# Filler work between lattice stretches regrouped, the gate convolution in four rounds, and one-column products spread over the array

## The chip, the cores and the metric

The kernel runs on one core of a Trainium2 chip. The metric is the device time of one execution in microseconds (us), as a median over runs. A core has a matrix engine (TensorE, PE in the profile; its weight loads are PEld), VectorE (DVE), ScalarE (ACT), GpSimd (POOL) and SyncE (SP), which here only issues DMAs. Each engine takes its instructions in the order of its own program, and they meet through semaphores.

## The reference

An image batch x of 32 x 8 x 256 x 256 goes through two layers, each added to its input.

```python
drive = x                        # layer 0 on group-normalised x
grid = drive
for _ in range(15):              # a coupled map lattice
    mapped = 3.9 * grid * (1.0 - grid)
    local = conv3x3(mapped, K_local, groups=8)
    physics = 0.7 * mapped + 0.3 * local
    grid = 0.85 * physics + 0.15 * drive
cml = clip(grid, 0.0001, 0.9999)
h = relu(conv3x3(x, Wp, bp))     # 8 -> 128 channels
nca = sigmoid(conv1x1(h, Wu, bu))
gin = concat([x, cml, nca])      # 24 channels
g = sigmoid(conv1x1(relu(conv3x3(gin, Wg1, bg1)), Wg2, bg2))
return g * cml + (1 - g) * nca
```

Layer 1 quantises its normalised input to whole numbers within 127, with one scale for the whole batch, and convolves it 3x3.

## The kernel before

Phase one does layer 0. Images go in eight groups of four. The lattice of a group is the main thread: for each of the 8 channels, two tiles (s = 0, 1; two images each) take 15 steps. One step of one tile is a **stretch** of TensorE work (`half`, lines 480 to 528), 240 in a group, 1920 in all. A stretch makes four blocks of float32 products, each on 64 x 64 tiles of the array: a diagonal product (low rows to low columns, high to high) and an off-diagonal one, into four blocks of two PSUM units. They go in four parts, in the order of line 501, off-diagonal of one block and diagonal of another in each, and after the first three parts `mark` (line 271) runs a product of one column. VectorE adds the drive (`gt`, line 510) and makes the next map (line 520). Two formats alternate (`m_a`, `m_b`). From `m_a` to `m_b` GpSimd clears edges (line 525); from `m_b` to `m_a` the rows at tile edges are exchanged by two DMAs on SP (`exchange`, lines 469 to 475), which the next stretch of the same tile waits for. A tile's next stretch comes two stretches later.

PE's order is written out by hand. The lattice yields after each stretch, and `together` (line 845) runs other generators in the gap until their yields, scaled by total weights, have caught up with the lattice's. These fillers are:

- `nca` (line 576): for each of 8 strips of an image, eight `hidden` pairs, each twelve products of `im` with `wp_hi` and `wp_lo` into `ph`, one unit of PSUM, and a relu on ScalarE to `h`. A `drain` (line 598) is four float32 products of `h` into `acc`. Per i there are two pairs, each with its own yield, and the drain of the i before. The four loads of the next strip (`rows`, line 561) are issued after the first pair of a strip.
- `gate` (line 705) of the group before: in each of 8 strips, `opened` (four products with `gw2`, then a sigmoid) for the strip before, then the 3x3 convolution of `gin` (x and cml rows, 96 partitions) and `gnc` (nca rows, 48 partitions): five column parts for each, four 32-column products a part, 40 in all (lines 760 to 768). `inputs` (line 656) loads the next strip with three DMAs. The mix, statistics and stores that belong to a strip are `chores`, of which `together` takes one per stretch.
- `prep` (normalising the next group), with products of one column (lines 323 and 356).

`both` (line 861) merges fillers by the same kind of weights; T_NCA, T_GATE, T_PREP and T_LATTICE (line 893) are the sums of the yields.

PSUM has three units of two banks in rotation: a stretch takes two, a pair or a gate strip one; `acc` and `mark` have one bank each. SP's queue holds, in program order, exchanges, up to four background loads or stores of the lattice after each stretch, and what the fillers issue.

Phase two does layer 1 from the stored result. When the lattice of the last group is over, the gate of its four images runs by itself first.

Of the kernel before, what the change touches and what calls it, by code (L numbers as in the profile page):

```python
# [40 lines left out]
P = 128  # L41
# [68 lines left out]
def kernel(  # L110
# [6 lines left out]
    wp: bass.AP,  # L117
    wu: bass.AP,
    wg1: bass.AP,
    wg2: bass.AP,  # L120
    w1: bass.AP,
    bp: bass.AP,
# [20 lines left out]
    grp = cp.tile([P, 4], F32, name="grp")  # L143
    mean_x = cp.tile([P, B, 4], F32, name="mean_x")
    rstd_x = cp.tile([P, B, 4], F32, name="rstd_x")
    gw = cp.tile([96, 2, 3, 32], F32, name="gw")
    gw2 = cp.tile([P, P], F32, name="gw2")
    qw = cp.tile([P, 3, P], BF16, name="qw")
    wp_hi = cp.tile([P, 3, HID], F32R, name="wp_hi")
# [16 lines left out]
    with tc.tile_pool(name="prep", bufs=1) as pp, tc.tile_pool(name="prep2", bufs=2) as pp2:  # L166
        kt = pp.tile([P, K_COLS], F32, name="kt")
        nc.sync.dma_start(kt, konst)
        nc.sync.dma_start(lw, kloc)
        kc = pp.tile([P, 3, P], F32, name="kc")  # L170
        nc.sync.dma_start(kc, kcen)
        nc.sync.dma_start(gw, wg1)
        g2 = pp.tile([P, C], F32, name="g2")
        nc.sync.dma_start(g2, wg2)
        wl = pp.tile([P, 72], F32, name="wl")
        nc.sync.dma_start(wl, w1)
        wp32 = pp.tile([P, 3, HID], F32, name="wp32")
        nc.sync.dma_start(wp32, wp)
        V.tensor_copy(wp_hi, wp32)
        V.tensor_tensor(wp_lo, wp32, wp_hi.bitcast(F32), ALU.subtract)  # L180
        G.memset(wu_z, 0.0)
        nc.sync.dma_start(wu_z[:, 24:32], wu)
        nc.sync.dma_start(bp_sb, bp)
        nc.sync.dma_start(bv, bvec)

        G.memset(zt, 0.0)
        borders = []
        for t, at, n, w, rows in (  # L190
            *((t, 0, 2 * C, W, ((0, 1), (257, 1))) for t in xp_s),
            *((t, j * PART, C, W, ((0, 1), (257, 1))) for t in gs_s for j in range(3)),
            *((t, 0, C, W, ((0, 1), (257, 5), (262, 5), (267, 1))) for t in y_s),
        ):
            k = 64
            for row, m in rows:
                borders.append(
                    (
                        dram_ap(t, at + row * n * w, [[w, m * n], [k, w // k], [1, k]]),
                        zt[: m * n, :k].unsqueeze(1).to_broadcast([m * n, w // k, k]),  # L200
                    )
                )
        for _ in range(2 * NBUF):
            nc.scalar.dma_start(*borders.pop(0))

        V.tensor_copy(masks, kt[:, K_MASK : K_MASK + 2])
        V.tensor_copy(junk, kt[:, K_JUNK : K_JUNK + 2])
        V.tensor_copy(grp, kt[:, K_GRP : K_GRP + 4])
        V.tensor_copy(sel, kt[:, K_SEL : K_SEL + P])
        G.memset(avg, 1.0 / P)  # L210
        G.memset(mhalf, -0.5)

        lin = -R_CML * (1.0 - BETA)
        V.tensor_scalar(kc, kc, lin * (1.0 - EPS_CML), None, ALU.mult)
        for c in range(C):
            V.scalar_tensor_tensor(lw[:, c], lw[:, c], lin * EPS_CML, kc, ALU.mult, ALU.add)

        def blocks(dst, src, off):  # L220

            for dy in range(3):
                t = kt[:, K_M + dy * P : K_M + (dy + 1) * P].rearrange("p (r o) -> p r o", o=C)
                w = src[:, off(dy) : off(dy) + C].unsqueeze(1).to_broadcast([P, 16, C])
                if dy == 0:
                    V.tensor_tensor(dst.rearrange("p (r o) -> p r o", o=C), t, w, ALU.mult)
                else:
                    tmp = pp2.tile([P, P], F32, name="tmp", tag="tmp")
                    V.tensor_tensor(tmp.rearrange("p (r o) -> p r o", o=C), t, w, ALU.mult)
                    V.tensor_tensor(dst, dst, tmp, ALU.add)  # L230

        V.tensor_tensor(
            gw2.rearrange("p (r o) -> p r o", o=C),
            kt[:, K_M + P : K_M + 2 * P].rearrange("p (r o) -> p r o", o=C),
            g2.unsqueeze(1).to_broadcast([P, 16, C]),
            ALU.mult,
        )


        wmax = pp.tile([P, 1], F32, name="wmax")  # L240
        V.tensor_reduce(wmax, wl, AX.X, ALU.max, apply_absolute_value=True)
        wall = pp.tile([P, 1], F32, name="wall")
        G.partition_all_reduce(wall, wmax, P, bass.bass_isa.ReduceOp.max)
        V.reciprocal(sw, wall)
        V.tensor_scalar(sw, sw, MAX_Q, None, ALU.mult)
        V.tensor_scalar(wl, wl, sw, None, ALU.mult)
        V.tensor_scalar(wl, wl, ROUND, ROUND, ALU.add, ALU.subtract)
        V.tensor_scalar(wl, wl, MAX_Q, -MAX_Q, ALU.min, ALU.max)
        for dx in range(3):
            t32 = pp2.tile([P, P], F32, name="t32", tag="t32")  # L250
            blocks(t32, wl, lambda dy: (dy * 3 + dx) * C)
            V.tensor_copy(qw[:, dx, :], t32)


    with ExitStack() as one:
# [12 lines left out]
        def unit():  # L268
            return ps_u.tile([P, 2, 512], F32, name="pt", tag="pt")

        def mark():

            one_ = ps_m.tile([P, 1], F32, name="mark", tag="mark")
            T.matmul(one_[HIGH], qw[HIGH, 0, HIGH], qw[HIGH, 0, 0:1], start=True, stop=True)  # L274

        fixed = lambda shape, name, dt=F32: np_.tile(shape, dt, name=name)
        hi, lo = fixed([P, 2, 2, W], "hi", F32R), fixed([P, 2, 2, W], "lo", F32R)
# [1 line left out]
        for t in ims:  # L279
            for w in (0, PW - 1):  # L280
                G.memset(t[:, :, :, w].bitcast(F32), 0.0)
        TU = 2 * NT
        m_a = [fixed([P, TU, NJ + 2], f"m_a{i}") for i in range(2)]
        m_b = [fixed([P, TU, NJ + 1], f"m_b{i}") for i in range(2)]
# [107 lines left out]
        def lattice(g):  # L392
# [87 lines left out]
            def half(c, step, s, d, m_a, m_b):  # L480
# [17 lines left out]
                    for src, dst, w, rhs in parts:  # L498
                        T.matmul(pt[dst], lw[src, c, w, dst], rhs[src], start=first, stop=not first)  # L499

                for o, dg, first in ((1, 0, True), (3, 2, True), (0, 1, False), (2, 3, False)):
                    blocks(o, False, first)
                    blocks(dg, True, first)
                    if (o, dg) != (2, 3):
                        mark()

                gts = []
                for pt, (ts, w) in zip(two, HALVES):
# [27 lines left out]
            for c in range(C):  # L536
                u = g * C + c
                for step in range(STEPS):
# [5 lines left out]
                    for s in range(2):  # L544
# [5 lines left out]
                            if u + 1 in units:  # L550
                                begin(units[u + 1], s)
                        background(4)
                        yield 2.05

            stored[g] = issued[0] + len(later)
            if g == NG - 1:
# [19 lines left out]
        def nca(b):  # L576
# [16 lines left out]
                S.activation(h.rearrange("p i c -> p (i c)"), ph.rearrange("p i c -> p (i c)"), AF.Relu, bias=bp_sb)  # L593
                return h[:, 0, :], h[:, 1, :]

            pend = done = None

            def drain():
                acc, t, i, hs = pend
                for g in range(4):  # L600
                    T.matmul(  # L601
                        acc[32 * g : 32 * g + 32], wu_z[:, 24 - 8 * i : 56 - 8 * i], hs[4 * g + i],
# [19 lines left out]
            for t in range(NT8):  # L622
                im = ahead
                acc = ps_a.tile([P, 512], F32, name="acc", tag="acc")
                for i in range(4):
                    hs = {}
                    for n in (i, i + 4):
                        hs[n], hs[n + 8] = hidden([im[64 * q : 64 * q + 48, :, n, :] for q in range(2)])
                        if n == 0:
                            if t < NT8 - 1:  # L630
                                ahead = rows(b, t + 1)
                            elif all((b + 1, g) in ready for g in range(4)):
                                loaded[b + 1] = rows(b + 1, 0)
                        yield 1.4
                    if i == 2 and done:
                        nc.sync.dma_start(*done)
                        done = None
                    if pend:
                        done = drain() or done
                    pend = (acc, t, i, hs)  # L640
                    yield 0.9
            done = drain()
            yield 0.9
            nc.sync.dma_start(*done)

        def scales(b):
# [9 lines left out]
        def inputs(b, t):  # L656

            src = gs_s[b % NBUF]
            gin = gip.tile([96, 8, W], F32, name="gin", tag="gin")
            gnc = gip.tile([48, 8, W], F32, name="gnc", tag="gnc")  # L660
            for j, to in enumerate((gin[:48], gin[48:], gnc)):
                nc.sync.dma_start(
                    to, dram_ap(src, j * PART + 32 * t * C * W, [[W, 48], [4 * C * W, 8], [1, W]])
                )
            return gin, gnc

        def blend(b, t):

# [36 lines left out]
        def gate(b):  # L705
# [38 lines left out]
            for t in range(NT8 + 1):  # L744
# [5 lines left out]
                    now["gt"] = opened(two[:, 1, :], last["r1"])  # L750
                    now["was"] = last
                if t < NT8:
                    (gin, gnc), mix = ahead
                    if t < NT8 - 1:
                        now["ahead"] = [inputs(b, t + 1)]
                    elif (b + 1) % GB:
                        staged[b + 1] = [inputs(b + 1, 0)]
                    pa = two[:, 0, :]
                    three = pa.rearrange("p (k w) -> p k w", w=W)
                    for j, src in enumerate((gin, gnc)):  # L760
                        rows_ = src.shape[0]
                        for n, (dx, to, of) in enumerate(PARTS):
                            for i in range(4):
                                T.matmul(  # L764
                                    three[32 * i : 32 * i + 32, :, to],
                                    gw[:rows_, j, dx, :], src[:, i::4, of],
                                    start=(j == 0 and n == 0), stop=(j == 1 and n == len(PARTS) - 1),
                                )
                    r1 = wk.tile([P, 512], F32, name="r1", tag="r1", bufs=1)
                    S.activation(r1, pa, AF.Relu, bias=bv[:, 0:1])  # L770
                    now["r1"], now["t"], now["mix"] = r1, t, mix
# [28 lines left out]
                if sums:  # L800
                    chores.append(sums.pop(0))
                last = now
                yield 2.3 if t < NT8 else 0.9
                while t < NT8 - 1 and len(now.get("ahead", ())) < 2 and chores:
                    chores.pop(0)()
                ahead = now.get("ahead")
# [81 lines left out]
        def after(g, gen):  # L888
# [1 line left out]
            while issued[0] < stored[g]:  # L890
                yield 4.0
            yield from gen
        T_NCA, T_GATE, T_PREP, T_LATTICE = 473.6, 77.2, 4.8, 8 * 30 * 2.05
        for _ in prep(0, ((0,),)):
            pass
        for g in range(NG):
# [181 lines left out]
```

## Time and profile before

| | us |
|---|---|
| median of 3 runs | 12336.9 (12310.65 to 12346.97) |
| the profiled execution | 12344.86 |
| its span, first to last instruction | 12343.1 |
| lattice group 0 (64 to 1533) | 1469 |
| lattice group 2 (2948 to 4371) | 1423 |
| lattice group 7 (10051 to 11379) | 1328 |
| gate after the lattice (11379 to 11769) | 390 |
| phase two (11798 to 12343) | 545 |

Busy time of an engine is the union of its instructions' records. A matmul's end is modelled, so a start is the safer mark. "a <- b: us, times, longest" in a list of waits says how long a sat idle and what ended it. In the timeline each row is a merged run of instructions: start, length, engine, line, operation, tiles, shape and count; a float32 product stands as two records. 64*64 64x320 is 64 rows by 64 columns of weights and 320 moving columns. The costliest groups of matmuls, busy us and mean ns of one:

```profile
L593 ACT ACTIVATE h<-pt,bp_sb 128x1024 f32<-128x1024 f32 x2048 | 2274.2, 1112 | 5042.4 <-PE pt L585 5032.7
L499 PE MATMUL pt<-m_a,lw 64*64 64x325 f32 (+1 forms) x30720 | 2404.9, 432 | 405.2 <-DMA m_a<-m_a 358.0
L585 PE MATMUL pt<-im,wp_hi 48*128 48x512 f32 x12288 | 2627.7, 424 | 144.7 <-ACT h L593 105.2
...
L601 PE MATMUL acc<-h,wu_z 128*32 128x512 f32 x8192 | 1107.0, 611 | 0.0
L764 PE MATMUL pt<-gin,gw 96*32 96x384 f32 (+2 forms) x10240 | 775.6, 452 | 197.2 <-ACT gate L716 181.2
L274 PE MATMUL mark<-qw 64*64 64x1 bf16 x5760 | 946.4, 164 | 0.0
L764 PE MATMUL pt<-gnc,gw 48*32 48x384 f32 (+2 forms) x10240 | 735.3, 430 | 0.0
```

### The profile page before, as it was taken

Reading aid. Unit: us, or ns where it says so; the run is one execution under the profiler, and the core shown is the slowest. Engines: PE = TensorE matmul, PEld = TensorE weight load, DVE = VectorE, ACT = ScalarE, POOL = GpSimd, SP = SyncE. Lnnn points to the kernel's source line nnn. Section 1 sums busy time; section 2 is a strip of 40 time slices with the busy share of each in tenths; the row PEclk is TensorE's granted clock in tenths of the full one; section 3 lists DMA queues with packets and bytes.
Section 4 is the critical chain, followed back from the end, with each engine's and each line's share of the span. In section 5 each row is a group of like instructions: output and inputs, shape, how many; then the busy total and the mean of one; then the engine's idle time right before and its main releaser. Section 6 shows DMA issues by size and latency. Waiting matters only on the chain. (4 is left out here: it accounts for less than half of the span.)

```text
span 12343.1 us, 289997 instructions
## 1 busy us (share of the span) xinstructions
PE 11018.7 (89%) x124192; PEld 6195.1 (50%) x124192; DVE 7823.5 (63%) x11376; ACT 3787.1 (31%) x4034; POOL 1577.6 (13%) x2242
## 2 busy tenths in 40 slices
PE   4888899999999999999999999999999999999854
PEld 2554555555555555555555555555555555555222
DVE  4555666666666666666666666666666666665377
ACT  2222233332333333333333333333333333332133
POOL 1000011111111111111111111111111111111300
PEclk7999999999999999999999999999999999999676
DMA  6545567766777667676776667677667666665988
GB/s 169 98 96 100 102 136 144 144 137 139 142 145 147 137 135 147 144 144 130 147 147 139 133 140 148 135 144 148 134 142 149 137 132 126 125 121 115 201 246 257
DMA packets 2473159, 1759.74 MB, mean 143 GB/s; under 512 B 1021280, under 2 KB 2442944, under 8 KB 2471744
## 3 DMA queue, kind: packets, MB, share of 16 engines
q1 hardware_dynamic: 2380096, 1651.64, 65.1%
q10 hardware_dynamic: 91776, 89.53, 2.3%
q8 instruction: 979, 16.04, 0.6%
q14 instruction: 308, 2.52, 0.1%
HBM read 1130.62 MB, written 473.89 MB: 130 GB/s over the span
## 5 line engine op out<-in xcount | busy, mean ns | idle before, releaser
L593 ACT ACTIVATE h<-pt,bp_sb 128x1024 f32<-128x1024 f32 x2048 | 2274.2, 1112 | 5042.4 <-PE pt L585 5032.7
L499 PE MATMUL pt<-m_a,lw 64*64 64x325 f32 (+1 forms) x30720 | 2404.9, 432 | 405.2 <-DMA m_a<-m_a 358.0
L585 PE MATMUL pt<-im,wp_hi 48*128 48x512 f32 x12288 | 2627.7, 424 | 144.7 <-ACT h L593 105.2
L510 DVE SCALAR_TENSOR_TENSOR gt<-pt,d_b 128x650 f32<-128x650 f32 (+1 forms) x1920 | 1463.6, 763 | 1987.5 <-PE mark L274 1350.7
L510 DVE SCALAR_TENSOR_TENSOR gt<-pt,d_a 128x640 f32<-128x640 f32 (+1 forms) x1920 | 1446.9, 754 | 1608.5 <-PE mark L274 1137.5
L585 PE MATMUL pt<-im,wp_lo 48*128 48x512 f32 x12288 | 2437.3, 393 | 0.0
L499 PE MATMUL pt<-m_b,lw 64*64 64x320 f32 (+1 forms) x30720 | 2305.8, 417 | 111.8 <-DVE gt L510 79.6
L499 PEld LDWEIGHTS pt<-m_a,lw 64*64 64x64 f32 x30720 | 1459.6, 137 | 1193.0 <-issue 511.4
L499 PEld LDWEIGHTS pt<-m_b,lw 64*64 64x64 f32 x30720 | 1380.3, 133 | 903.0 <-issue 451.6
L585 PEld LDWEIGHTS pt<-im,wp_hi 48*128 48x128 f32 x12288 | 1160.8, 185 | 1250.9 <-issue 730.9
L520 DVE SCALAR_TENSOR_TENSOR m_a<-gt 128x640 f32<-128x640 f32 (+1 forms) x1792 | 1429.2, 798 | 58.6
L520 DVE SCALAR_TENSOR_TENSOR m_b<-gt 128x650 f32<-128x650 f32 (+1 forms) x1792 | 1384.3, 774 | 100.6 <-DVE gt L510 1.8
L525 POOL TENSOR_TENSOR m_b<-m_b,junk 128x36 f32<-128x36 f32 x896 | 243.5, 272 | 8070.3 <-DVE m_b L520 5355.6
L585 PEld LDWEIGHTS pt<-im,wp_lo 48*128 48x128 f32 x12288 | 1166.4, 186 | 201.1
L601 PE MATMUL acc<-h,wu_z 128*32 128x512 f32 x8192 | 1107.0, 611 | 0.0
L764 PE MATMUL pt<-gin,gw 96*32 96x384 f32 (+2 forms) x10240 | 775.6, 452 | 197.2 <-ACT gate L716 181.2
L274 PE MATMUL mark<-qw 64*64 64x1 bf16 x5760 | 946.4, 164 | 0.0
L764 PE MATMUL pt<-gnc,gw 48*32 48x384 f32 (+2 forms) x10240 | 735.3, 430 | 0.0
L764 PEld LDWEIGHTS pt<-gin,gw 96*32 96x32 f32 x10240 | 313.3, 115 | 823.7 <-issue 422.0
L687 POOL TENSOR_TENSOR d<-mix 128x256 f32<-128x256 f32 x512 | 554.2, 1099 | 1254.1 <-DVE gate L722 866.6
L274 PEld LDWEIGHTS <-qw 64*64 64x64 bf16 x5760 | 631.5, 110 | 137.0 <-issue 0.6
L764 PEld LDWEIGHTS pt<-gnc,gw 48*32 48x32 f32 x10240 | 295.0, 109 | 423.0 <-issue 416.3
(110 smaller groups left out, 5940.8 us busy)
## 6 DMA issues: line engine op xcount, KB each, us to landing
im<-xp_s SPq DMA_DIRECT2D x1024, 384.0 KB
gin<-gs_s SPq DMA_DIRECT2D x512, 384.0 KB
mix<-gs_s SPq DMA_DIRECT2D x512, 384.0 KB
gnc<-gs_s SPq DMA_DIRECT2D x256, 384.0 KB
d_a<-gs_s SPq DMA_DIRECT2D x2048, 36.0 KB
yb<-y_s ACTq DMA_DIRECT2D x28, 2432.0 KB
xr<-in_x_dram SPq DMA_DIRECT2D x128, 512.0 KB
xp_s<-hi SPq DMA_DIRECT2D x256, 256.0 KB
```

The costliest lines, as they stand in the source:

```text
L274: T.matmul(one_[HIGH], qw[HIGH, 0, HIGH], qw[HIGH, 0, 0:1], start=True, stop=True)
L499: T.matmul(pt[dst], lw[src, c, w, dst], rhs[src], start=first, stop=not first)
L510: V.scalar_tensor_tensor(gt.rearrange("p (u c) -> p u c", u=2), pt[:, :, : w * n], FLOOR, d[:, ts, :].rearrange("p (u t) j -> p u (t j)", ...
L520: V.scalar_tensor_tensor(to, gt, 1.0, gt, ALU.subtract, ALU.mult)
L525: G.tensor_tensor(edge, edge, junk.unsqueeze(1).to_broadcast([P, TU, 2]), ALU.mult)
L585: T.matmul(ph[:, i, :].rearrange("p (h w) -> p h w", w=W), w[64 * i : 64 * i + 48, dx, :], rhs[:, :, dx : dx + W], start=(dx == 0 and w is ...
L593: S.activation(h.rearrange("p i c -> p (i c)"), ph.rearrange("p i c -> p (i c)"), AF.Relu, bias=bp_sb)
L601: T.matmul(acc[32 * g : 32 * g + 32], wu_z[:, 24 - 8 * i : 56 - 8 * i], hs[4 * g + i], start=(i == 0), stop=(i == 3),)
L687: G.tensor_tensor(d[:, cols], mix[:, 1, k], mix[:, 2, k], ALU.subtract)
L764: T.matmul(three[32 * i : 32 * i + 32, :, to], gw[:rows_, j, dx, :], src[:, i::4, of], start=(j == 0 and n == 0), stop=(j == 1 and n == le ...
```

## The change

Four edits go together.

1. Marks: the three one-column products of a stretch run on three tiles of the array, in place of one.
2. `nca`: both pairs of an i are one piece with one yield, and the drains of two i are one piece after every second i. The next strip's loads follow the second pair.
3. Gate: all 128 partitions of `gin` are filled (48 rows of x, 48 of cml, the first 32 of nca). The last 16 nca rows go to `gl`, loaded five times over with the shift in columns already made, so that 48 partitions hold the three shifts and one product replaces five parts: 24 products for 40. `inputs` issues eight DMAs for three.
4. The weights of the yields are changed: 2.4 for a stretch, 2.9 for two pairs, 1.9 for two drains, 4.5 for a gate strip, and the totals with them.

```diff
-        def mark():
+        MARKS = ((HIGH, HIGH), (LOW, LOW), (LOW, HIGH))
+        def mark(n):
+            src, dst = MARKS[n]
             one_ = ps_m.tile([P, 1], F32, name="mark", tag="mark")
-            T.matmul(one_[HIGH], qw[HIGH, 0, HIGH], qw[HIGH, 0, 0:1], start=True, stop=True)
+            T.matmul(one_[dst], qw[src, 0, dst], qw[src, 0, 0:1], start=True, stop=True)
...
+        gls = [fixed([48, 8, W], f"gl{i}") for i in range(2)]
+        for t in gls:
+            for w in (0, W - 1):
+                G.memset(t[:, :, w], 0.0)
...
-                for o, dg, first in ((1, 0, True), (3, 2, True), (0, 1, False), (2, 3, False)):
+                for n_, (o, dg, first) in enumerate(((1, 0, True), (3, 2, True), (0, 1, False), (2, 3, False))):
                     blocks(o, False, first)
                     blocks(dg, True, first)
-                    if (o, dg) != (2, 3):
-                        mark()
+                    if n_ < len(MARKS):
+                        mark(n_)
...
-                        yield 2.05
+                        yield 2.4
...
                     for n in (i, i + 4):
                         hs[n], hs[n + 8] = hidden([im[64 * q : 64 * q + 48, :, n, :] for q in range(2)])
-                        if n == 0:
-                            if t < NT8 - 1:
-                                ahead = rows(b, t + 1)
-                            elif all((b + 1, g) in ready for g in range(4)):
-                                loaded[b + 1] = rows(b + 1, 0)
-                        yield 1.4
-                    if i == 2 and done:
-                        nc.sync.dma_start(*done)
-                        done = None
-                    if pend:
-                        done = drain() or done
-                    pend = (acc, t, i, hs)
-                    yield 0.9
-            done = drain()
-            yield 0.9
+                    pend.append((acc, t, i, hs))
+                    if i == 0:
+                        if t < NT8 - 1:
+                            ahead = rows(b, t + 1)
+                        elif all((b + 1, g) in ready for g in range(4)):
+                            loaded[b + 1] = rows(b + 1, 0)
+                    yield 2.9
+                    if i % 2:
+                        if done:
+                            nc.sync.dma_start(*done)
+                            done = None
+                        while pend:
+                            done = drain(*pend.pop(0))
+                        yield 1.9
...
-            gin = gip.tile([96, 8, W], F32, name="gin", tag="gin")
-            gnc = gip.tile([48, 8, W], F32, name="gnc", tag="gnc")
-            for j, to in enumerate((gin[:48], gin[48:], gnc)):
+            gin = gip.tile([P, 8, W], F32, name="gin", tag="gin")
+            for j, (lo_, hi_) in enumerate(((0, 48), (48, 96), (96, P))):
                 nc.sync.dma_start(
-                    to, dram_ap(src, j * PART + 32 * t * C * W, [[W, 48], [4 * C * W, 8], [1, W]])
+                    gin[lo_:hi_],
+                    dram_ap(src, j * PART + 32 * t * C * W, [[W, hi_ - lo_], [4 * C * W, 8], [1, W]]),
                 )
-            return gin, gnc
+            gl = gls[(NT8 * b + t) % 2]
+            for dx, to, of in PARTS:
+                nc.sync.dma_start(
+                    gl[16 * dx : 16 * dx + 16, :, to],
+                    dram_ap(src, 2 * PART + (32 * t + 4) * C * W + of.start,
+                            [[W, 16], [4 * C * W, 8], [1, of.stop - of.start]]),
+                )
+            return gin, gl
...
-                    for j, src in enumerate((gin, gnc)):
-                        rows_ = src.shape[0]
-                        for n, (dx, to, of) in enumerate(PARTS):
-                            for i in range(4):
-                                T.matmul(
-                                    three[32 * i : 32 * i + 32, :, to],
-                                    gw[:rows_, j, dx, :], src[:, i::4, of],
-                                    start=(j == 0 and n == 0), stop=(j == 1 and n == len(PARTS) - 1),
-                                )
+                    for n, (dx, to, of) in enumerate(PARTS):
+                        for i in range(4):
+                            T.matmul(
+                                three[32 * i : 32 * i + 32, :, to],
+                                gw[:, dx, :], gin[:, i::4, of], start=(n == 0), stop=False,
+                            )
+                    for i in range(4):
+                        T.matmul(
+                            three[32 * i : 32 * i + 32], gwl, gl[:, i::4, :], start=False, stop=True
+                        )
...
-                yield 2.3 if t < NT8 else 0.9
+                yield 4.5 if t < NT8 else 0.9
...
-        T_NCA, T_GATE, T_PREP, T_LATTICE = 473.6, 77.2, 4.8, 8 * 30 * 2.05
+        T_NCA, T_GATE, T_PREP, T_LATTICE = 32 * 15.4, 4 * (8 * 4.5 + 0.9), 4.8, 8 * 30 * 2.4
```

The rest of the diff moves the weights: `gw` has 128 partitions and the small weights of `gl` come as one more input, `wg1l`, into `gwl`.

## The prediction

> **What bounds the kernel now.** I read the page's engine list first, then busy time by stage, then what TensorE waits for in one stage, then the order of its matmuls. Every time below belongs to the profiled execution (span 12343.1 us, run 12344.86 us); it lies 8 us over the median of the three runs, 12336.9 us.
>
> ```profile
> PE 11018.7 (89%) x124192; PEld 6195.1 (50%) x124192; DVE 7823.5 (63%) x11376; ACT 3787.1 (31%) x4034; POOL 1577.6 (13%) x2242
> ```
>
> By stage (columns: span, busy us of each engine, granted clock, DMA share, GB/s): the first row is lattice group 0, the next two are of the six groups that have lattice, nca, gate and prep side by side, the last is the gate work left when the lattice is over.
>
> ```profile
> 64.00:1533.00 1469.00, 1174.99 (x12612) 708.41 (x12616) 842.10 (x1291) 407.37 (x389) 112.82 (x168) 0.89 0.53 110
> 2948.00:4371.00 1423.00, 1328.60 (x15392) 752.96 (x15384) 922.01 (x1380) 446.61 (x464) 199.01 (x276) 0.98 0.70 141
> 11379.00:11769.00 390.00, 326.14 (x3061) 111.09 (x3056) 147.03 (x235) 76.83 (x105) 116.06 (x140) 0.71 0.85 190
> ```
>
> In a full group TensorE is busy 1329 of 1423 us. Its waits there are few:
>
> ```profile
> PE pt L499 <- DMA m_a<-m_a: 31.5, 18, 7.0
> PE pt L764 <- ACT gate L716: 22.9, 28, 0.9
> PE pt L585 <- ACT h L593: 15.0, 12, 1.9
> PE pt L499 <- DVE gt L510: 13.3, 13, 3.7
> ```
>
> So a full group costs what its matmuls cost in a row, plus some 94 us. Group 0 and the tail are different: TensorE is idle a fifth of group 0 (142 us of it on m_a exchanges, clock 0.89), and in the tail the DMA engines are at 0.85.
>
> **Price of the pieces.** I take a piece from its first matmul to the first matmul of the next piece, so the change of tile shape is in it.
>
> ```profile
> 6045.74 0.98 PE L499 MATMUL pt<-m_b,lw 64*64 64x320 f32 x11
> ...
> 6048.02 1.06 PE L714 MATMUL pt<-r,gw 128*32 128x512 f32 x8
> 6049.89 2.79 PE L764 MATMUL pt<-gin,gw 96*32 96x512 f32 x40 [0.81 <-ACT gate L716]
> 6052.61 2.78 PE L764 MATMUL pt<-gnc,gw 48*32 48x512 f32 x40
> 6055.32 0.98 PE L499 MATMUL pt<-m_b,lw 64*64 64x320 f32 x11
> ...
> 6057.60 0.50 PE L585 MATMUL pt<-im,wp_hi 48*128 48x512 f32 x2
> ...
> 6059.18 0.99 PE L499 MATMUL pt<-m_a,lw 64*64 64x325 f32 x11
> ```
>
> A lattice stretch (L) is 2.28 here, 2.31 in the other format (mean 2.29); opening a gate and waiting for its sigmoid 1.87; the two convolution halves 2.72 and 2.71; one ph pair (H) 1.58, median 1.60. Two pieces of one kind in a row occur too:
>
> ```profile
> 5911.54 0.50 PE L585 MATMUL pt<-im,wp_hi 48*128 48x512 f32 x2
> ...
> 5914.55 0.99 PE L499 MATMUL pt<-m_a,lw 64*64 64x325 f32 x11
> ```
>
> ```profile
> 2218.18 1.92 PE L601 MATMUL acc<-h,wu_z 128*32 128x512 f32 x16
> 2220.04 0.77 PE L499 MATMUL pt<-m_b,lw 64*64 64x320 f32 x8
> ```
>
> Two H together: 3.01, not 3.20, so 0.18 less. Two drains (A): 1.86, against 2 x 1.00 (median of the single ones), so 0.14 less.
>
> **Order.** Following the generators' yields against the lattice's gives the order of pieces. For the old weights it gives 1432 runs of one H and 994 single A; the trace has 1416 and 994, so I trust it. In a full group of 240 stretches, old: 216 runs of H, 126 of A, 2 stretches with nothing between. New: 128 runs of H (all double), 64 of A (all double), 31 empty gaps; the commonest pair of neighbouring gaps is HH, A.
>
> **The sum for a full group.**
> 1. Gate convolution. The gnc half (five parts, 2.71) becomes four f32 products of 512 columns in the same 32-column form as a drain: 1.00. So 1.72 less a batch; 30 of its 32 batches stand between stretches: **-52**. The wait for ACT's gate (0.9) stays: opened still comes first and shares a unit.
> 2. H runs: 88 fewer x 0.18 = **-16**. A runs: 62 x 0.14 = **-9**.
> 3. Empty gaps: two stretches met without a piece took 4.47 at 6140.23, not 2 x 2.29: 29 x 0.10 = **-3**.
> 4. Marks. All three run on the (HIGH, HIGH) tile. In the stretch at 6004.61 single records show that tile's second part 0.065 behind the other three after the first mark, 0.13 after the second, 0.19 at the end (last pass 6006.581 against 6006.39); the next piece waits for it. Spread, each tile has at most one, so 0.065 remains: 0.12 x 240 = **-29**. Bounds: 0 if the lateness only moves to other tiles, -46 if it vanishes.
>
> The Trainium skill (TensorE: Matmul & The Clock Gate, Part 3, The mechanism) says matmuls start strictly in program order; by that a late tile holds all, spreading gains nothing, and the sum is 29 smaller a group. The trace differs: at 6005.202 to 6005.214 three tiles start products that stand behind the mark, which starts at 6005.221.
>
> Together -109 of work. **What is late next** is the exchange of m_a. An odd stretch must be written by VectorE, sent by two SP DMAs, and land before the same lattice's next stretch, two stretches on:
>
> ```profile
> 6008.82 0.69 DVE L520 SCALAR_TENSOR_TENSOR m_a<-gt 128x512 f32<-128x512 f32 x1
> 6009.58 0.60 SPq L474 DMA_DIRECT2D m_a<-m_a  x1
> 6010.22 0.60 SPq L475 DMA_DIRECT2D m_a<-m_a  x1
> ```
>
> From the stretch's start (6004.61) that is 6.2 us to the second issue's end. In the DMA records the last of its 2112-byte packets ends 7.3 (lower quartile), 7.9 (median), 9.3 (upper), 11.0 (nine tenths) after that start, and a waiting matmul follows 0.85 later. What the order gives it, two stretches and two gaps: old, 10.2 median and 8.6 at the lowest twentieth; new, 9.2 (2 x 2.17 + 3.01 + 1.86) and 7.2 (one gap empty). Averaging the shortfall of every such pair against that distribution gives 58 us a group before and 94 after. TensorE's measured wait on m_a was 31.5, 0.55 of the 58, so the rise is between 0.55 x 36 and 36: +20 to +36.
>
> Around it: inputs issues 8 DMAs for 3. Five more at about 0.49 (other loads of this size) put 2.5 us on SP a batch, ahead of the next exchange and of the background loads behind it; SP waits 437 us a group on VectorE for m_a, which covers the 80, but where a gate stands between two exchange stretches the second goes out about a microsecond late: +12. Their 640 packets, less 128 of gnc, cost 16 engines about 1.3 us a batch at 22 ns for 256 bytes and 76 for 1024 (0.70 of DMA time becomes about 0.76). The im issues now follow the second pair, not the first, and nca's store its double drain: their count is unchanged and SP passes them in the same gaps. VectorE takes 3.0 a stretch; with an empty gap behind a gate, two stretches (6.0) and the mix (0.69 + 1.13) do not fit 7.3 of TensorE: +10. I take **+50** of new waits; bounds 0, and +100 if every exchange lands 2 us later (shortfall 228, at 0.55 of its rise, and the rest).
>
> So -59 a group, over groups 1 to 7: **-410**. Group 0 has no gate work; 57 of saved product time meet a group that exchanges and the low clock hold at 12.2 us per pair of stretches: -10, from -57 to +60. The tail is held by a load per batch that grows by an eighth: 0, from -54 (1.7 x 32) to +30. One more setup load and four memsets: 1 us. Phase two (545 us) is untouched. Span 12343 - 419 = 11924; at the median's distance, **11918 us**.
>
> **Rivals.**
> - *The waits don't grow* (the old waits sit at a few unit ends, longest 7.0): 7 x 109 + 10 off, **11570**. Against it: one pair of gaps in eight falls below what an undisturbed exchange needs.
> - *Spreading the marks gains nothing*: -30 a group, **12120**. For it, only the tile's own lateness is measured, not what another tile's mark delays.
> - *Slower: the exchange becomes the bound.* More packets and SP issues just where gaps empty out. It decides once new waits pass 109 a group, about 2 us more on each of 112 exchanges. At 3 us: shortfall 319, rise 261 x 0.55 = 144: +35 a group, **12580**. For it: DMA 0.76 busy, nine-tenths landing at 11 us. Against it: quiet landings at 7.3.
> - *The order does not come out as listed*, because H or A wait for ACT where pairs meet: between 12250 and 12400.
>
> **Chances.** Forecast 0.66, no new waits 0.07, marks without gain 0.13, slower 0.10, order 0.04. The forecast's own range is 11700 to 12100. Above 12230 lies the slower rival, below 11640 about half of the no-wait case: 11640 to 12230 leaves some 0.17 out. What can be told from no change is 0.3%, 37 us. Faster 0.86, same 0.04, slower 0.10.
>
> **What would show it.** Stretches of 2.17; 24-matmul runs of 3.0 and 16-matmul runs of 1.86; conv from first product to the next stretch 3.71; TensorE's wait on m_a in a full group 50 to 70 us, not 31; full groups near 1360. It is wrong if stretches stay at 2.29, if m_a waits pass 140 a group, or if gl's loads hold the convolution.

## The result and the profile after

The changed kernel takes 12453.7 us (median of 4 runs, 12450 to 12470) against 12333.9 before: ratio 1.010 [1.008, 1.012], slower. The profiled execution's span is 12448.0 us.

The page's engine line of the changed kernel:

```profile
PE 10421.0 (84%) x116000; PEld 6023.5 (48%) x116000; DVE 7703.9 (62%) x11376; ACT 3798.3 (31%) x4034; POOL 1574.5 (13%) x2246
```

TensorE has 598 us less of busy time and 8192 fewer records, and the span is 105 us longer. By stage, in the columns of the prediction's rows (group 0, group 2, the gate behind the lattice):

```profile
64.00:1431.00 1367.00, 1113.03 (x12608) 694.46 (x12608) 825.81 (x1287) 407.95 (x386) 113.84 (x168) 0.91 0.57 118
2888.00:4326.00 1438.00, 1260.09 (x14376) 732.83 (x14372) 906.30 (x1380) 447.60 (x465) 200.26 (x276) 0.94 0.73 145
11489.00:11874.00 385.00, 237.96 (x1949) 77.30 (x1941) 139.26 (x235) 73.94 (x102) 99.93 (x140) 0.74 1.06 216
```

Group 0, which has no gate, became 102 us shorter. The six full groups (1 to 6) each became 13 to 41 us longer (30 on average; group 2, shown here, 15), and their clock fell from 0.98 to 0.94. In the stage behind the lattice TensorE's busy time fell from 326 to 238 us and the span by 5 alone: its waits for gin's loads there rose from 16 to 115 us. What TensorE waits for in group 2:

```profile
PE pt L509 <- DMA m_a<-m_a: 115.0, 36, 14.0
PE pt L780 <- ACT gate L734: 23.8, 28, 2.0
PE pt L595 <- DVE gt L520: 13.6, 30, 1.6
```

One wait grew by far the most: that of a stretch for its exchange, from 31.5 to 115 us in this group, 358 to 968 us in all. SP's own timeline shows where one of the long ones comes from:

```profile
2828.89 2.24 SPq L576 DMA_DIRECT2D im<-xp_s  x4
2831.16 3.56 SPq L669 DMA_DIRECT2D gin<-gs_s  x3
2834.77 9.04 SPq L675 DMA_DIRECT2D gl<-gs_s  x5
2846.68 0.65 SPq L484 DMA_DIRECT2D m_a<-m_a  x1
2848.80 0.64 SPq L485 DMA_DIRECT2D m_a<-m_a  x1
```

The last of VectorE's `m_a` rows were written at 2840.1; the exchange behind the five gl loads was issued at 2846.7. The five, 0.5 us each when SP is free, took 9 us. By the semaphores in the trace, SP's DMAs carry eight of them in turn, and each DMA waits until the one eight places before it has landed. The third gl load waits for the semaphore of the second im load, and so on; the exchange itself waits for the first gin load, which was issued at 2831.2 and landed at 2846.6. Meanwhile the DMA engines were full (share 1.14, in the last column but one of this row):

```profile
2832.00:2843.00 11.00, 11.00 (x145) 6.77 (x145) 8.50 (x12) 4.18 (x6) 1.99 (x4) 1.00 1.14 148
```

This meeting of loads is not the rule but a coincidence of the order: in 55 of the 256 strips the gate's loads follow directly on the four im loads. There the five gl loads take 8.7 us (median; 2.35 at the lower quarter of all strips), and within 30 us each of the 55 is followed by a wait on m_a of over 5 us, 414 us of the 968 in all. TensorE's timeline at the same place:

```profile
2841.74 1.92 PE L610 MATMUL acc<-h,wu_z 128*32 128x512 f32 x16
2852.22 1.79 PE L509 MATMUL pt<-m_a,lw 64*64 64x325 f32 x11 [8.56 <-DMA m_a<-m_a]
...
2853.45 1.53 PE L509 MATMUL pt<-m_a,lw 64*64 64x260 f32 x7
```

It waits 8.56 us, and then a part of a stretch that takes 0.99 elsewhere takes 1.79: the clock has been halved, as the granted clock behind the wait shows (third column from the end):

```profile
2852.00:2857.00 5.00, 4.78 (x37) 3.00 (x39) 1.21 (x2) 0.00 (x0) 0.00 (x0) 0.50 0.67 207
```

In group 2 the granted clock was 0.5 for 60 us before and 160 us after. The Trainium skill (TensorE: Matmul & The Clock Gate, Part 1, What's actually happening) says that an idle window of some 3.4 us brings the half clock. This wait agrees: it began at 2843.66, and the clock record goes to 0.5 at 2846.97. TensorE was busy in 52 and 115 us of the 60 and 160, so by an estimate from these figures the half clock cost it some 31 us more in this group.

### The profile page after: what moved, and what is told of

Read it like the earlier page. It is cut to its first block, busy times and chain, and to the rows that moved or that the text cites. A ratio compares the mean times of both kernels' runs of the same rounds, so it can differ in the third digit from the quotient of the medians.

```text
span 12448.0 us, 275007 instructions
## 1 busy us (share of the span) xinstructions
PE 10421.0 (84%) x116000; PEld 6023.5 (48%) x116000; DVE 7703.9 (62%) x11376; ACT 3798.3 (31%) x4034; POOL 1574.5 (13%) x2246
## 5 line engine op out<-in xcount | busy, mean ns | idle before, releaser
L509 PE MATMUL pt<-m_a,lw 64*64 64x325 f32 (+1 forms) x30720 | 2479.1, 460 | 1005.0 <-DMA m_a<-m_a 968.2
L595 PE MATMUL pt<-im,wp_hi 48*128 48x512 f32 x12288 | 2596.1, 418 | 130.8 <-DVE gt L520 111.6
L595 PE MATMUL pt<-im,wp_lo 48*128 48x512 f32 x12288 | 2473.4, 398 | 0.0
L509 PE MATMUL pt<-m_b,lw 64*64 64x320 f32 (+1 forms) x30720 | 2184.7, 413 | 74.7 <-ACT h L603 46.9
L509 PEld LDWEIGHTS pt<-m_b,lw 64*64 64x64 f32 x30720 | 1246.7, 133 | 790.3 <-issue 329.7
L610 PE MATMUL acc<-h,wu_z 128*32 128x512 f32 x8192 | 1043.6, 606 | 0.7 <-issue 0.7
L780 PE MATMUL pt<-gin,gw 128*32 128x384 f32 (+2 forms) x10240 | 790.8, 458 | 280.5 <-ACT gate L734 165.6
L780 PEld LDWEIGHTS pt<-gin,gw 128*32 128x32 f32 x10240 | 322.6, 117 | 910.1 <-issue 552.8
L610 PEld LDWEIGHTS acc<-h,wu_z 128*32 128x32 f32 x8192 | 224.9, 110 | 551.8 <-issue 516.9
L703 ACT ACTIVATE f<-mix,sc 128x512 f32<-128x512 f32 x256 | 208.6, 815 | 831.9 <-DVE y L741 498.5
```

Of the source, the lines that this page charges most:

```text
L595: T.matmul(ph[:, i, :].rearrange("p (h w) -> p h w", w=W), w[64 * i : 64 * i + 48, dx, :], rhs[:, :, dx : dx + W], start=(dx == 0 and w is ...
L610: T.matmul(acc[32 * g : 32 * g + 32], wu_z[:, 24 - 8 * i : 56 - 8 * i], hs[4 * g + i], start=(i == 0), stop=(i == 3),)
L703: S.activation(f, flat(mix[:, 0]), AF.Identity, bias=sc[:, 0:1], scale=sc[:, 2:3])
L780: T.matmul(three[32 * i : 32 * i + 32, :, to], gw[:, dx, :], gin[:, i::4, of], start=(n == 0), stop=False,)
```

## The experiments

Ratios are against the kernel before, with 95% intervals. "Wait" is TensorE's on the m_a exchange, in us over the whole execution (358 before, 968 in the changed kernel).

**First round: which edit, and by what.**

```diff
# e1_marks: before, with edit 1 (marks) alone
# e2_gate: before, with edit 3 (gin of 128, gl) alone, yields as before
# e3_old_gate: the change without edit 3
# e4_gl_one: the change, and
-            for dx, to, of in PARTS:
-                nc.sync.dma_start(gl[16 * dx : 16 * dx + 16, :, to], ...)
+            nc.sync.dma_start(gl, dram_ap(src, 2 * PART + 32 * t * C * W, [[W, 48], [4 * C * W, 8], [1, W]]))
```

> The kernel before with the marks alone spread over three tiles. All theories agree on the work: a stretch of 2.16 to 2.19 us in place of 2.28 to 2.31, as in the changed kernel's trace, so 0.12 x 1920 = 230 us less at most (ratio 0.981). Theory A (slots: SP's DMAs take eight semaphores in turn and each waits until the DMA eight places before it has landed, so the five gl loads behind im and gin hold SP, and the next m_a exchange with it) and theory C (traffic: the gl packets slow everything) expect nearly all of it, 0.980 to 0.986, with TensorE's wait on m_a rising from 358 to 400 to 500 us. Theory B (order: any work taken from between two stretches comes back as a wait, since the exchange needs its time) expects less than half, 0.991 or more.

> The kernel before with the gate convolution of the change (gin of 128 partitions, gl, eight loads for three), and the order and weights of the yields as before. Work: 1.72 x 256 = 440 us less at most. Theory A (slots) expects that much of it is lost, since the eight loads are there: wait on m_a above 700 us, ratio 0.985 to 1.01. Theory B (order) expects most of the gain, since single pieces and nearly no empty gaps remain: 0.968 to 0.978, wait on m_a under 500. Theory C (traffic) goes with A here.

> The changed kernel with the gate convolution and the three loads of before; marks, double pieces and the new weights of the yields stay. Work left out: 230 (marks) + 131 (H runs) + 68 (A runs) us less than before at most. Theory A (slots) and C (traffic) expect a clear gain over before: 0.968 to 0.982, wait on m_a 400 to 600 us. Theory B (order) expects it no faster than before: 0.998 to 1.02, wait on m_a 800 or more.

> The changed kernel with one load into all 48 partitions of gl (393 KB, 384 packets of 1024 bytes) in place of five (392 KB, 640 packets), so the gate sums lack the column shifts of the last 16 nca rows. Same bytes, four slots fewer. Theory A (slots) expects wait on m_a to fall from 968 to under 550 us and a ratio of 0.960 to 0.980. Theory C (traffic in bytes) and theory B (order) expect little change from the changed kernel: 0.998 to 1.012.

| | ratio | wait |
|---|---|---|
| e1_marks | 0.992 [0.989, 0.994] | 414 |
| e2_gate | 1.023 [1.021, 1.026] | 849 |
| e3_old_gate | 0.997 [0.996, 0.999] | 516 |
| e4_gl_one | 1.002 [1.000, 1.003] | 901 |

No theory fits all four. The gate edit alone, which takes 440 us of products out, makes the old kernel 2.3% slower, in the old order of pieces: so the new order is not what costs most, but the time is worse than any theory allowed. e3 has the wait that theories A and C expected and nearly the time of theory B: with the gate of before, the other edits keep 0.3% of some 430 us of products, so the gate's loads are not the whole either. Marks give 104 us of 230: the stretch is 2.16 to 2.19, but part of it comes back elsewhere, as B said. e4 is the telling one. With four DMAs fewer, SP stands behind im far less ahead of gl:

```profile
SPq L675 <- DMA im<-xp_s: 605.0, 352, 3.5
```

is the changed kernel's wait ahead of gl, and this is e4's:

```profile
SPq L674 <- DMA im<-xp_s: 104.2, 56, 2.3
```

Yet the wait on m_a fell by 67 us only. The exchange was now issued in time more often (over 1 us late at 41 of the 672 exchanges of the full groups, against 176), but its last packet ended late: from the second issue's end, nine tenths of them within 6.3 us, against 3.5 in the changed kernel. The queue had moved from SP's semaphores into the DMAs in flight. The 55 meetings of im and gate loads are still there, and cost 403 us of waits on m_a as against 414. So the slots are a part (0.8% in time), not the cause.

**Second round: the backlog.**

```diff
# e5_exch_pool: the change, and in exchange()
-                nc.sync.dma_start(...)
+                nc.gpsimd.dma_start(...)
# e6_im_spread: the change, and in nca(); rows() returns im and its four loads
-                            ahead = rows(b, t + 1)
+                            ahead, todo = rows(b, t + 1)
+                    if todo:
+                        nc.sync.dma_start(*todo.pop(0))
                     yield 2.9
# e7_all_spread: e6, and the eight gin and gl loads dealt out over the next five chores
# e8_conv_short: the change, with three loads a strip
+            for j, to in enumerate((gin[:48], gin[48:96], gl)):
...
+                                gw[:96, dx, :], gin[:96, i::4, of], start=(n == 0), stop=False,
```

> The changed kernel with the two m_a exchange DMAs of a stretch issued from GpSimd's queue in place of SP's. Theory D (backlog: the exchange stands behind bulk loads in SP's order, in its eight semaphores or in its DMA queue) expects the exchange to pass them: TensorE's wait on m_a falls from 968 to under 400 us and the ratio is 0.955 to 0.975. Theory R (the DMA engines themselves are full in those moments, so any queue waits) expects wait on m_a above 800 us and 1.00 to 1.02. GpSimd's own issue is an unknown price: if it takes over 2 us a pair, D's gain is smaller.

> The changed kernel with the four im loads of a strip issued one after each of the four double pairs, in place of four in a row. Same DMAs, same bytes, same order of products. Theory D (backlog) expects the wait on m_a to fall from 968 to 600 to 800 us and a ratio of 0.985 to 1.000. Theory P (the exchange needs 8 us even on an empty queue, and the gaps are too short for it) expects no change from the changed kernel, 1.006 to 1.012.

> As e6_im_spread, and the eight gin and gl loads of a gate strip are issued one or two after each of the next five stretches, in place of eight in a row. Theory D (backlog) expects the wait on m_a under 500 us and a ratio of 0.960 to 0.980, which would be faster than both kernels. Theory P expects 1.00 to 1.01.

> The changed kernel's products with the loads of before: three gate loads (x and cml rows into gin, 48 nca rows into gl), 24 products a strip, the first 20 on 96 rows, so the gate sums lack most of the nca rows. Against e3_old_gate (0.997), which has the same loads and order, it only takes 1.72 us of products out of each gate gap. If the extra loads are what costs, the 30 x 7 batches give 360 us and the ratio is 0.965 to 0.975. If the old length of the gate gap was the cover under which bulk loads and the exchange landed (cover theory), the gap's time comes back as wait on m_a, which rises from 516 to 750 us or more, and the ratio stays at 0.985 to 1.000.

| | ratio | wait |
|---|---|---|
| e5_exch_pool | 1.061 [1.059, 1.063] | 1396 |
| e6_im_spread | 0.968 [0.966, 0.970] | 193 |
| e7_all_spread | 1.029 [1.027, 1.032] | 557 |
| e8_conv_short | 0.983 [0.980, 0.985] | 704 |

e6 moves nothing but im's loads: the second to fourth of a strip come some 17, 23 and 26 us later (medians), and the kernel is 4.2% faster than the changed one. No gate load follows on four im loads in it any more. Two of the longest sums of TensorE's waits in it:

```profile
PE pt L595 <- DMA im<-xp_s: 241.3, 76, 15.6
```

```profile
PE pt L509 <- DMA m_a<-m_a: 192.6, 150, 7.0
```

The wait on m_a is a fifth of what it was; a new one has come, for the fourth im load (75 of the 76 times), which was issued too late. e5 speaks against the simple form of theory D: on another queue the exchange does not pass the bulk loads. It is issued 0.5 us after VectorE's write in nine cases of ten, in 0.56 us of GpSimd's time, but it lands late:

```profile
DMA to landing us min/median/max: 1.8/4.3/11.3
```

The trace tells whether the DMA engines were full or the other queue is slower by itself. Where bulk loads held under 0.3 of the engines meanwhile, the exchange's last packet ended 2.15 us (median) after its first issue, as against 2.29 on SP's queue in the changed kernel; where they held over 0.8, it took 7.4 us, as against 5.1 on SP's. So it is the full engines that make the exchange late, as theory R has it, though R expected a ratio of 1.00 to 1.02; why it became 1.061 no run shows. e7 failed for every theory: dealt out over all gaps, the gate's loads stand within eight places of 485 of the 672 exchanges of the full groups (310 in the changed kernel), and the first issue was more than 1 us late at 204 of them, against 176 in the changed kernel and 69 in e6. That spreading helps only where a load then stands in front of no exchange is argued from this, not shown. e8 lies between its two cases: by the ratios of e3 and e8, some 180 of 360 us of products come through once the loads are those of before.

**Third round: without the burst.**

```diff
# e9_im_early: e6, with two, one, one and no loads behind the four double pairs
+                    for _ in range((2, 1, 1, 0)[i]):
                         if todo:
# e10_before_im: before, im loads one behind each of the first four pairs
# e11_old_gate_im: e3 with e9's im loads
# e12_marks_im: e10 with edit 1
```

> As e6_im_spread (0.968, where TensorE now waits 241 us for the last im load), but two im loads follow the first double pair, one the second and one the third. Theory D (backlog) expects the wait on im to fall under 80 us with the wait on m_a at 200 to 400 us, and a ratio of 0.955 to 0.966. If two loads in a row already hold the exchange up, the two waits swap and the ratio stays at 0.966 to 0.975.

> The kernel before, with its four im loads issued one after each of the first four pairs of a strip instead of together after the first; nothing else. Theory D (backlog) expects that the kernel before already lost its 358 us of waits on m_a to this burst: under 180 us, ratio 0.975 to 0.988. If the burst only matters where the gaps are short, the ratio is 0.995 to 1.003.

> The changed kernel with the gate convolution and the three gate loads of before, and im spread as in e9_im_early: it differs from e9 in the gate alone. The products cost 440 us more than e9's. If the gate's five more loads cost little once the burst is gone, it is 0.02 to 0.03 slower than e9, 0.980 to 0.995; if they still take what the shorter convolution gives, it is within 0.008 of e9 or faster.

> e10_before_im with the marks spread. Alone on the kernel before, the marks gave 94 to 139 us of their 230 (0.9916). Theory D (backlog) expects that with the burst gone they give 180 to 230 us, 0.015 to 0.019 below e10. If the exchange's own 8 us bounds the order (theory P), they give no more than before, 0.006 to 0.011 below e10.

| | ratio | wait |
|---|---|---|
| e9_im_early | 0.944 [0.942, 0.945] | 407 |
| e10_before_im | 0.981 [0.979, 0.983] | 197 |
| e11_old_gate_im | 0.947 [0.945, 0.949] | 149 |
| e12_marks_im | 0.973 [0.971, 0.975] | 245 |

e9 holds the whole change with nothing left out and takes 11642 us, less than both kernels; of the trials below, e13 and e14 are faster, but e13 leaves out the column shifts of the last nca rows and e14 most nca rows of the convolution. e9's group 2 (2706 to 4044):

```profile
2706.00:4044.00 1338.00, 1230.76 (x14372) 720.31 (x14368) 907.06 (x1380) 447.94 (x464) 202.58 (x276) 0.98 0.76 156
```

The clock is back at 0.98, at 156 GB/s in place of 145. e10 shows that the burst already cost the old kernel 1.9%. On that footing the marks give 0.9 points (about 105 us), no more than before: half of their 230 us comes back, 48 of it as wait on m_a (197 to 245; the profiled execution of e12 lay 43 us above its median, so this part is uncertain). Theory D expected more here. The double pieces and the new weights of the yields are worth most, about 2.6 points (e11 against e12, which also differ a little in where the im loads stand). Beside them the gate edit is worth 0.4 (e9 against e11).

**Fourth round: why the gate edit yields so little.**

```diff
# e13_im_gl_one: e9 with e4's single gl load
# e14_im_conv_short: e9 with e8's loads and products
# e15_im_gl_late: e9, the five gl loads as the last chore of a strip
+                steps += [lambda now, f=f: f() for f in late]
# e16_im_gl_second: e15, the same chore as the second
+                steps[1:1] = [lambda now, f=f: f() for f in late]
```

> e9_im_early (0.944) with one load into all 48 partitions of gl in place of five, so the gate sums lack the column shifts of the last 16 nca rows. Same bytes, four DMAs fewer a strip. If the number of loads holds the exchange (theory A, slots), the wait on m_a falls from 407 to under 250 us and the ratio to 0.925 to 0.936. If it is the bytes or the shorter gap, the ratio stays at 0.940 to 0.946.

> e9_im_early with the three gate loads of before (48 nca rows into gl) and 24 products a strip, the first 20 on 96 rows, so the gate sums lack most nca rows. Loads as in e11 (0.947), products as in e9. If loads alone eat the gain, the 360 us of products beside the lattice come through: 0.916 to 0.928, wait on m_a under 220 us. If the shorter gap is time that the exchange needs anyway (cover theory), 0.935 to 0.945 with the wait above 350 us.

> e9_im_early with the five gl loads of a strip issued as the last of its chores, some five stretches later, the three gin loads staying at the strip. It computes the reference. If eight loads in a row are what holds the exchange, wait on m_a falls from 407 to 200 to 320 us and the ratio to 0.930 to 0.940, the best of all. If any load between two exchanges costs the same wherever it stands, 0.942 to 0.955.

> e15_im_gl_late (0.973) with the five gl loads as the second chore of a strip, one or two stretches behind the gin loads and not five. It computes the reference. If e15 lost only because gl landed late (314 us of TensorE's wait), that wait is under 30 us here and the ratio is 0.930 to 0.943, at or below e9 (0.944). If loads between other exchanges cost as much there, 0.944 to 0.956.

| | ratio | wait |
|---|---|---|
| e13_im_gl_one | 0.938 [0.935, 0.941] | 374 |
| e14_im_conv_short | 0.924 [0.922, 0.926] | 252 |
| e15_im_gl_late | 0.973 [0.971, 0.976] | 328 |
| e16_im_gl_second | 0.947 [0.945, 0.950] | 365 |

e14 against e11 has the same loads and 1.72 us of products less a strip: 2.35 points, some 290 us of the 360 beside the lattice. So the shorter convolution is worth its price where its loads are not longer. The cover theory falls in the main; the wait on m_a does rise, from 149 to 252 us. e13 shows that four DMAs fewer give back 0.6 points, and the rest between e13 and e14 (1.4 points) goes with one more DMA and 256 KB a strip (1408 against 1152). In e15 the loads came too late for the products that want them:

```profile
PE pt L799 <- DMA gl<-gs_s: 314.2, 83, 7.9
```

In e16, one or two stretches behind gin, they cost as much as beside it: TensorE waits for gl no more, but 87 us for im. No place tried for the five loads is better than the change's own.

## Why the prediction was wrong

The time forecast was 11918, range 11640 to 12230; measured 12454. Going through its steps:

- **Prices of the pieces: right.** Median stretches of 2.16 and 2.19 (2.17), double pairs 3.01, double drains 1.86, convolution 3.71. In the trace all 1024 double pairs stand as listed, and 30 batches a group between stretches, with 32 gaps empty of fillers' pieces but prep's (31 forecast).
- **Marks: right in size, wrong in worth.** Each stretch lost its 0.12 us, so the lateness does stay on one tile of the array; e1 and e12 turn 230 us of it into about 105.
- **Waits: the step that failed.** The forecast had "**+50** of new waits; bounds 0, and +100" a full group. In group 2 the idle time of TensorE rose by 84 (94 to 178 us), over the six full groups by 93 on average. Besides, busy time fell by 69 and not by 109: some 31 us of the rest went into the half clock, a cost that the prediction did not have at all, and 9 stay unexplained. So -69 + 84 = +15 stands in place of -59, and groups 1 to 7 together grew by 212 us instead of shrinking by 410. Two sentences inside the step failed. "Five more at about 0.49 (other loads of this size) put 2.5 us on SP a batch" priced an issue by its length on a free SP; that holds where nothing stands ahead (2.35 at the lower quarter), but in a row behind seven bulk loads five took 9 us, since each waited for a landing. And im's loads were passed over as unchanged in count, though e6, e9 and e10 show that their standing in a row is what the exchange waits for, most of all right before gin and gl.
- **The distribution of landings** was taken from the old trace and shifted by the order alone. It belongs to how loads and products met there: with the gate's loads longer and the gaps shorter its upper tenth went from some 11 to some 14 us, and in e11, with the gaps as short but the loads of before and im's apart, it is 8.6.
- **Group 0**: -10 forecast, -102 measured. e1 has 1459 us there and e3 1361, so it is the double pieces and the new weights that brought it, in a group taken to be held by exchanges. Why they help there so much was not tried. For the forecast this is luck: without it the time would have been off by 92 us more.
- **Tail**: 0 forecast, -5 measured (390 to 385), with the DMA engines full (share 1.06) and the time of the products turned into waits for gin, as the forecast had it.
- **The slower rival** had the mechanism (exchange as the bound, by SP issues and packets where gaps shrink) and 12580; it was given 0.10. It was priced by 2 to 3 us more on every exchange; in truth few waits of 5 to 15 us made most of it: 62 of over 5 us hold 478 of 745 us in the six full groups, ten a group.
- The sign that should have shown the forecast wrong, m_a waits over 140 a group, was set too high: 115 in group 2 sufficed, since less of the work had come out than the sum took for granted.

## What to carry to other kernels

Where a short latency-bound DMA shares the DMA engines with bulk loads, products taken out of the gaps are worth little until the bulk loads no longer stand in a row before it: the same products gave 0.3% in e3 and, with im's loads apart, 5.3% in e11. Look for what is issued ahead of it, count the DMAs in flight and their bytes, and move the loads before cutting work. Price an added DMA by the landing that it makes the queue wait for and by its bytes, not by its issue time alone. A wait of several microseconds on TensorE costs a second time through the halved clock (in group 2 by estimate 31 us beside 84).

## What the runs showed of the hardware

- SP's DMAs here went through eight semaphores in turn: the ninth waited for the landing of the first, so five issues took 9.04 us in place of 2.5.
- Products on different 64 x 64 tiles of the array run past a late tile: a stretch with one one-column product on each of three tiles is 0.12 us shorter than with three on one.
- The same exchange from GpSimd's queue landed 4.3 us after its issue (median) beside SP's bulk loads; it did not get ahead of them. What made it late was full DMA engines: 2.15 us to the last packet where bulk loads held under 0.3 of them, 7.4 where they held over 0.8.
